# A logarithm in SBUF, its add on GpSimd, and the front's steps placed anew in a selective-scan loop

## The chip, the cores and the metric

The kernel runs on one core of a Trainium2 chip. A core has a matrix engine (TensorE, PE in the profile; PEld are its weight loads), VectorE (DVE), ScalarE (ACT), GpSimd (POOL) and SyncE (SP), which here issues most of the DMAs. Each engine works through its own queue in order; engines wait for each other through semaphores. The metric is the device time of one execution in microseconds.

## The reference

The whole program is a two-layer model; the part that the change touches is the Mamba block of the first layer. For each of four groups of 64 channels (`nb`) and each of four images (`b`) it computes, over 1024 positions:

```
xz = xs @ inw.T
u, z = jnp.split(xz, 2, axis=-1)
u = silu(causal depthwise conv of u, 4 taps)
xdbc = u @ xpw.T
dt = softplus(xdbc[..., :4] @ dtw.T + dtb)
Bm, Cm = xdbc[..., 4:20], xdbc[..., 20:36]
dA  = exp(dt[..., None] * A)
dBu = (dt * u)[..., None] * Bm[:, :, None, :]
h_t = dA_t * h_(t-1) + dBu_t ;  y_t = sum over 16 states of h_t * C_t ;  y = y + u * D
out = y * silu(z) @ outw.T
```

There are 128 inner channels with 16 states each. Everything behind it (gates, depthwise convolutions, attention, a second attention layer, a mixture of experts) is the same in both kernels.

## The kernel before, in words

The work is cut into 16 blocks, one for each pair of group and image, in the order of `order` (all groups of image 0, then image 1, and so on). A block has 128 channels x 16 states = 2048 recurrences, and a tile has 128 partitions, so a block is 16 steps; in one step eight channels with their 16 states fill the partitions and the 1024 positions lie along the free axis. The loop runs over `t` from 0 to 259; `n = t // 16` is the block and `j = t % 16` the step.

One step does this:

- SP loads `dA` (`fetch`, L905): eight rows of dt from DRAM, each spread over 16 partitions. There are five buffers; the load for step t+4 is issued in step t.
- ScalarE takes its exponential in place (`decay`, L910), three steps ahead.
- TensorE writes dt*u, spread in the same way, into one of two PSUM buffers `dBu` (`select`, L917), two steps ahead. dt*u is held as three bf16 parts in `U`.
- VectorE multiplies it by B (L975) and runs the recurrence with `tensor_tensor_scan` (L978) into `hs`, which has six buffers.
- GpSimd multiplies `hs` by C (L979).
- TensorE sums over the states into `pY` (`add_up`, L928 for steps 0, 1, 14 and 15 of a block, L935 for pairs of the others, L941 for u*D), three steps behind. `pY` is a PSUM tile of 4 KB per partition, and its pool has one buffer: the first sum of a block (step 0's, issued in step 3 of the block) is the first write to the tile in which the block before collected its result.

Around these steps the loop places the work of other blocks. `front(n)` returns the steps that prepare block n, each with a number: a step with number i >= 0 is issued in step i of block n-1, one with i < 0 in step 16+i of block n-2. They are: the projection and convolution as matmuls (`project`, four parts, L484), `silu` (L488), the matmul for dt (`project_dt`, L495), softplus in pieces that avoid a large exponential (`exps`: Abs, Relu, Exp, and 1+e into the PSUM tile, L500 to L503; `rest`: VectorE's correction, L506, and GpSimd's subtraction, L507; `log`, L510; `dt_out`: the last add, L513, the store of dt to DRAM, L515, and e = dt*u, L516), the three bf16 parts of dt*u (`part1`, `part2`, L520 to L526), B and C spread over the partitions by matmul and copied by ScalarE (`spread`, L542 and L544), the store of the parts (`parts_out`, L530) and their load in another layout (`turn`, L537).

The loop itself also places the work on block n-1's result: `gated` (ScalarE copies `pY` into `u`, L566), `times_gate` (GpSimd multiplies by silu(z), L569), `project_out` (L579, L580), `store` (L585), and for block n `gate` (silu(z), L557 and L559). `module_gate` and `module` (L598 to L614) apply a gate to finished images.

PSUM is full during the loop: two `dBu` buffers, one `pY` and one buffer called `mm`, which all the other matmuls share in turn, of two banks each. The order of the instructions on every engine is the order in which the loop issues them (`tc.manual_schedule`); semaphores come from the tiles' reads and writes, and a tile's buffer passes on to the next tile of its name when all who read or write the old one are done. Ahead of the loop a planner (`Plan`) interleaves the normalisation and block 0's own front; it also issues the first five steps of front 1. Its list of engines, costs and keys decides the order there.

Of the kernel before, what the change touches and what calls it, by code (L numbers as in the profile page):

```python
# [10 lines left out]
F32 = mybir.dt.float32  # L11
BF16 = mybir.dt.bfloat16
AF = mybir.ActivationFunctionType
ALU = mybir.AluOpType
# [4 lines left out]
N = HH * WW  # L19
NP = N + 2  # L20
P = 128
CT = C // P
NT = N // P
NB, DM, DIN, DS, DTR, K = 4, 64, 128, 16, 4, 4
# [371 lines left out]
def body(tc, g, out):  # L396
    nc = tc.nc
    act, mm = nc.scalar.activation, nc.tensor.matmul
    ts, tt, stt = nc.vector.tensor_scalar, nc.vector.tensor_tensor, nc.vector.scalar_tensor_tensor
# [6 lines left out]
    with pool("const", 1) as cp, pool("dram", 1, space=bass.MemoryType.DRAM) as drp, contextlib.ExitStack() as late:  # L406
# [16 lines left out]
        def V(name, j=0, n=1):  # L423
            return vec[:, VOFF[name] + j : VOFF[name] + j + n]
# [26 lines left out]
        order = [(nb, b) for b in range(B) for nb in range(NB)]  # L451
        NBLK = NJ * len(order)
        with pool("mconst", 1) as mc, pool("front", 1) as fp, pool("dts", 2, space=bass.MemoryType.DRAM) as dsp, pool(
            "mps", 1, space=PSUM
        ) as mps:
            m_cu = mc.tile([P, CT, K, DIN], F32, tag="m_cu", name="m_cu")
# [8 lines left out]
            def block(nb, b):  # L465
                q0 = (nb % 2) * DM
                return slice(q0, q0 + DM), XM[b][q0 : q0 + DM, nb // 2]

            def big():
                return mps.tile([P, N], F32, tag="mm", name="mm")  # L470

            def front(n):


                nb, b = order[n]
                rows_in, xb = block(nb, b)
                r = state[n] = {}

                def project(part):
                    if part == 0:  # L480
                        r["pu"] = big()
                    h = HALVES[part // 2]
                    for k in range(part % 2 * 2, part % 2 * 2 + 2):
                        mm(r["pu"][:, h], m_cu[rows_in, nb // 2, k], xb[:, k + h.start : k + h.stop], start=k == 0, stop=k == K - 1)  # L484

                def silu():
                    r["u"] = fp.tile([P, N], F32, tag="u", name="u", bufs=3)
                    act(r["u"], r["pu"], AF.Silu, bias=V("convb", nb), scale=1.0)  # L488

                def project_dt():
                    r["pdt"] = big()
                    for h in HALVES:
                        mm(r["pdt"][:, h], m_wdt[:, nb, :], r["u"][:, h], start=True, stop=True)  # L495

                def exps():
                    e = r["e"] = fp.tile([P, N], F32, tag="e", name="e")
                    dt = r["dt"] = fp.tile([P, N], F32, tag="dt", name="dt")
                    act(e, r["pdt"], AF.Abs, bias=V("dtb", nb), scale=1.0)  # L500
                    act(dt, r["pdt"], AF.Relu, bias=V("dtb", nb), scale=1.0)
                    act(e, e, AF.Exp, scale=-1.0)
                    act(r["pdt"], e, AF.Identity, bias=one, scale=1.0)  # L503

                def rest():
                    stt(r["e"], r["pdt"], -1.0, r["e"], ALU.add, ALU.subtract)  # L506
                    nc.gpsimd.tensor_tensor(r["dt"], r["dt"], r["e"], ALU.subtract)  # L507

                def log():
                    act(r["pdt"], r["pdt"], AF.Ln)  # L510

                def dt_out():
                    tt(r["dt"], r["dt"], r["pdt"], ALU.add)  # L513
                    r["ds"] = dsp.tile([NJ, DB, N], F32, tag="ds", name="ds")
                    nc.sync.dma_start(out=r["ds"].rearrange("j d n -> (j d) n"), in_=r["dt"])  # L515
                    nc.gpsimd.tensor_tensor(r["e"], r["dt"], r["u"], ALU.mult)  # L516

                def part1():
                    p = r["parts"] = fp.tile([P, 3, N], BF16, tag="parts", name="parts")
                    nc.scalar.copy(p[:, 0], r["e"])  # L520
                    nc.gpsimd.tensor_tensor(r["e"], r["e"], p[:, 0], ALU.subtract)

                def part2():
                    p = r["parts"]
                    nc.scalar.copy(p[:, 1], r["e"])
                    nc.gpsimd.tensor_tensor(p[:, 2], r["e"], p[:, 1], ALU.subtract)  # L526

                def parts_out():
                    dq = r["dq"] = dsp.tile([P, 3, N], BF16, tag="dq", name="dq")
                    nc.sync.dma_start(out=dq, in_=r["parts"])  # L530

                def turn():

                    dq = r["dq"]
                    U = r["U"] = fp.tile([96, 4, N], BF16, tag="U", name="U", bufs=2)
                    for q in range(3):
                        nc.sync.dma_start(out=U[32 * q : 32 * q + 32], in_=dq.rearrange("(t c) q n -> q c t n", c=32)[q])  # L537

                def spread(c):
                    p = big()  # L540
                    for h in HALVES:
                        mm(p[:, h], m_bc[:, nb, c * P : (c + 1) * P], r["u"][:, h], start=True, stop=True)  # L542
                    t = r["BC"[c]] = fp.tile([P, N], F32, tag=f"bc{c}", name=f"bc{c}", bufs=2)
                    nc.scalar.copy(t, p)  # L544

                return [(i - 5, lambda i=i: project(i)) for i in range(4)] + [
                    (-1, silu), (0, project_dt), (1, exps), (3, rest), (4, log), (5, dt_out), (6, part1),
                    (6, lambda: spread(0)), (7, part2), (7, lambda: spread(1)), (10, parts_out), (12, turn),
                ]

            def gate(n):
# [66 lines left out]
            with pool("scan", 6) as sp, pool("yps", 1, space=PSUM) as yps, pool("dps", 2, space=PSUM) as dps, pool("lnA", 1) as wp:  # L618
# [50 lines left out]
                def XN(b, ks=range(CT), hs=range(2)):  # L669
                    return [("xn", b, k, h) for k in ks for h in hs]  # L670
# [272 lines left out]
                fronts = [front(n) for n in range(1, len(order))]  # L943
                fronts = [None] + fronts
# [15 lines left out]
                with pre.beside(-1, -1, -1, low=True):  # L960
                    for b in range(1, B):
                        normalise(b)
                    for i, step in fronts[1]:
                        if i < 0:
                            add("PE" if i < -1 else "ACT", 1720 if i < -1 else 1150, step, XN(0, [0]) + ["m_cu"], ["mm"])

                with tc.manual_schedule():
                    pre.run()
                with tc.manual_schedule():
                    for t in range(NBLK + 4):  # L970
                        n, j = t // NJ, t % NJ
                        if t < NBLK:
                            r = state[n]
                            dBu = dBus.pop(t)
                            tt(dBu, dBu, r["B"], ALU.mult)  # L975

                            hs = hss[t] = sp.tile([P, N], F32, tag="hs", name="hs")
                            nc.vector.tensor_tensor_scan(hs, dAs.pop(t), dBu, 0.0, ALU.mult, ALU.add)  # L978
                            nc.gpsimd.tensor_tensor(hs, hs, r["C"], ALU.mult)  # L979
                        if j == 3 and n > 0:  # L980
                            gated(n - 1)
                        select(t + 2)
                        add_up(t - 3)
                        fetch(t + 4)
                        decay(t + 3)
                        for ahead in (1, 2):
                            if n + ahead < len(order):
                                for i, step in fronts[n + ahead]:
                                    if i == j - (ahead - 1) * NJ:
                                        step()  # L990
                        for i, step in behind:
                            if i == t:
                                step()
                        if 0 < n < len(order) and j == 4:
                            times_gate(n - 1)
                        last = n == len(order)
                        for i in range(2):
                            if n > 0 and j == (3 if last else 8 + i):
                                project_out(n - 1, i)
                        if n > 0 and j == (3 if last else 9):  # L1000
                            store(n - 1)
                        if not last and j == 10:
                            gate(n)
                        if n > NB and j == 5 and n % NB > 0:
                            module_gate(n // NB - 1, n % NB - 1)
                        if n > NB and j == 8 and n % NB > 1:
                            module(n // NB - 1, n % NB - 2)


# [12 lines left out]
        with pool("sets", 1) as wp, pool("work", 1) as kp, pool("ps2", 1, space=PSUM) as ps:  # L1022
# [45 lines left out]
            add = plan.add  # L1068
# [1044 lines left out]
```

## Time and profile before

| what | value |
|---|---|
| median of the runs | 2809.41 us (2807.25 to 2810.01, 3 runs) |
| profiled execution | 2797.35 us, span of its instructions 2795.4 us |
| mean granted TensorE clock | 0.966 |
| busy over the span | PE 2525.0, DVE 2018.1, ACT 1540.3, POOL 1285.7 us |
| first scan of block 0, 1, 15 | 89.42, 157.75, 994.14 us |
| blocks 1 to 14, first scan to first scan | 836.39 us, mean 59.74, shortest 58.69 |
| L513 (the add that is moved) | 15 times, 1.19 us each |
| landing of a DMA, median | dA 4.7, ds 3.0, parts 5.8, U 5.9 us |

A line of a group is: source line, engine, operation, what it writes and reads, how often, then busy time and mean duration in ns, then the idle time of the engine just before and who ended it. A line of the order in time is: start and length in us, engine, source line, operation, and in square brackets the idle time before it with its releaser. A line of waits is: who waited for whom, us in total, times, longest. A line of stretches is: start and end, length, then busy time and number of instructions of PE, PEld, DVE, ACT and POOL, then granted clock, share of DMA time and GB/s.

### The profile page before, as it was taken

What the parts mean: (1) busy time and instruction counts of PE and PEld (TensorE: products, weight loads), DVE (VectorE), ACT (ScalarE), POOL (GpSimd) and SP (SyncE); (2) the same over time, 40 slices, a digit from 0 to 9 for tenths busy, and PEclk for the clock granted to TensorE, in tenths of its full rate; (3) what the DMA queues carried; (4) which work ended last, traced back from release to release, by engine and by line L of the source; (5) the groups of instructions that cost most, each with busy time, mean ns of one, the idle gap of its engine ahead of it and who ended that gap; (6) DMA issues with size and microseconds to landing.
All of it is one profiled execution on the core that took longest, in us unless ns stands there. A gap on an engine that the chain in (4) does not pass through costs nothing. (4 is left out here: it accounts for less than half of the span.)

```text
span 2795.4 us, 38909 instructions
## 1 busy us (share of the span) xinstructions
PE 2525.0 (90%) x15320; PEld 1490.3 (53%) x15320; DVE 2018.1 (72%) x2276; ACT 1540.3 (55%) x2082; POOL 1285.7 (46%) x807
## 2 busy tenths in 40 slices
PE   7788888888888878999899999998999997999996
PEld 5322222222222223676655656664666676899996
DVE  6899999999999996877995997777594566111112
ACT  4766666766676743776875975775443433111110
POOL 1688788887887870000010020012343436666652
PEclk9989999999999989999999999999999999999998
DMA  4667766776666653000001000000000013555546
GB/s 147 158 164 183 174 168 179 185 184 168 173 173 173 183 133 106 5 9 22 22 1 39 8 3 9 9 17 16 1 16 8 8 32 116 181 140 140 127 98 181
DMA packets 95433, 269.58 MB, mean 96 GB/s; under 512 B 18694, under 2 KB 36726, under 8 KB 91920
## 3 DMA queue, kind: packets, MB, share of 16 engines
q1 hardware_dynamic: 66560, 202.52, 27.3%
q0 software_dynamic: 26512, 60.35, 8.4%
q10 hardware_dynamic: 2176, 4.19, 0.4%
q8 instruction: 122, 2.00, 0.3%
q14 instruction: 63, 0.52, 0.1%
HBM read 291.57 MB, written 42.80 MB: 120 GB/s over the span
## 5 line engine op out<-in xcount | busy, mean ns | idle before, releaser
L979 POOL TENSOR_TENSOR hs<-hs,bc 128x1024 f32<-128x1024 f32 x256 | 600.8, 2354 | 157.7 <-DVE hs L978 154.1
L978 DVE TENSOR_TENSOR_SCAN hs<-dA,dBu 128x1024 f32<-128x1024 f32 x256 | 585.4, 2287 | 37.1 <-PE pY L935 6.8
L1321 DVE TENSOR_REDUCE nm<-s 128x1 f32<-128x1024 f32 x256 | 301.5, 1218 | 93.0 <-PE s L1312 91.5
L910 ACT ACTIVATE dA<-dA,aneg 128x1024 f32<-128x1024 f32 x256 | 286.6, 1144 | 96.5 <-DMA dA<-ds 81.6
L1326 ACT ACTIVATE pr<-s,nm 128x1024 f32<-128x1024 f32 x256 | 285.4, 1121 | 96.0 <-DVE nm L1321 71.2
L975 DVE TENSOR_TENSOR dBu<-dBu,bc 128x1024 f32<-128x1024 f32 x256 | 309.8, 1210 | 10.3 <-PE dBu L917 10.3
L1390 POOL TENSOR_TENSOR b<-b 128x1024 f32<-128x1024 f32 (+1 forms) x15 | 29.6, 1971 | 591.1 <-ACT b L1386 591.1
L1340 PE MATMUL k<-const,pr 128*128 128x128 f32 x2048 | 270.3, 279 | 21.5 <-ACT pr L1326 6.2
L1340 PEld LDWEIGHTS k<-const,pr 128*128 128x128 f32 x2048 | 226.4, 142 | 110.8 <-issue 49.4
L917 PE MATMUL dBu<-U,pick 96*128 96x512 bf16 x512 | 160.5, 397 | 113.9 <-DVE hs L978 113.7
L1988 PE MATMUL s<-pT,b 128*128 128x128 f32 x1920 | 231.2, 277 | 6.3 <-DMA b<-we,intse 5.8
L1988 PEld LDWEIGHTS s<-pT,b 128*128 128x128 f32 x1920 | 227.0, 193 | 11.5 <-issue 6.0
L935 PE MATMUL pY<-hs,const 128*32 128x512 f32 x768 | 215.0, 687 | 0.0
L1992 DVE TENSOR_TENSOR pT<-pT,s 128x512 f32<-128x512 f32 x72 | 49.3, 685 | 229.3 <-ACT pT L1991 229.1
L917 PEld LDWEIGHTS <-pick 96*128 96x128 bf16 x512 | 40.3, 98 | 290.2 <-issue 170.7
L1344 ACT COPY pT<-k 128x512 f32<-128x512 f32 x288 | 156.5, 597 | 51.4 <-PE k L1340 51.1
L1344 DVE COPY pT<-k 128x512 f32<-128x512 f32 x224 | 144.9, 682 | 34.0 <-PE k L1340 31.8
L1312 PE MATMUL s<-b,b 32*128 32x512 f32 x512 | 166.6, 644 | 0.7 <-ACT pr L1326 0.6
L1312 PE MATMUL s<-b,qs 32*128 32x512 f32 x512 | 166.6, 644 | 0.0
L1360 PEld LDWEIGHTS k<-pT,b 128*32 128x32 f32 x4096 | 108.0, 111 | 58.2 <-issue 26.8
L928 PE MATMUL pY<-hs,const 128*128 128x512 f32 x256 | 122.3, 600 | 12.2 <-ACT u L566 9.0
L1360 PE MATMUL k<-pT,b 128*32 128x128 f32 x4096 | 130.2, 276 | 3.0 <-DVE pT L1344 3.0
(485 smaller groups left out, 4636.3 us busy)
## 6 DMA issues: line engine op xcount, KB each, us to landing
dA<-ds SPq DMA_DIRECT2D x256, 512.0 KB, 4.7
dq<-parts SPq DMA_DIRECT2D x15, 768.0 KB, 5.8
U<-dq SPq DMA_DIRECT2D x45, 256.0 KB, 5.9
ds<-dt SPq DMA_DIRECT2D x16, 512.0 KB, 3.0
b<-x SPq DMA_DIRECT2D x4, 1024.0 KB, 6.6
acc<-pr SPq DMA_DIRECT2D x8, 512.0 KB, 8.6
qs<-b SPq DMA_DIRECT2D x32, 128.0 KB, 2.2
xm<-x SPq DMA_DIRECT2D x4, 1024.0 KB, 5.2
```

The source lines that it names most:

```text
L910: act(dAs[t], dAs[t], AF.Exp, scale=aneg[:, c : c + 1])
L935: mm(r["pY"][32 * q : 32 * q + 32, h], strip[:, P - DB - i * DB : P - i * DB + 32 - DB], hs[:, h], start=False, stop=False,)
L975: tt(dBu, dBu, r["B"], ALU.mult)
L978: nc.vector.tensor_tensor_scan(hs, dAs.pop(t), dBu, 0.0, ALU.mult, ALU.add)
L979: nc.gpsimd.tensor_tensor(hs, hs, r["C"], ALU.mult)
L1312: mm(S[i][:, HALVES[h]], q, kT[rr, HALVES[h]], start=True, stop=True)
L1321: "DVE", 1130, lambda i=i, u=u: nc.vector.tensor_reduce(nms[u], S[i], AX.X, ALU.max, negate=True),
L1326: "ACT", 1100, lambda i=i, u=u, hd=hd: act(prs[u % 4], S[i], AF.Exp, bias=nms[u], scale=1.0, accum_out=rss[b % 2][:, k, qt, hd : hd + 1]), ...
L1340: nc.tensor.transpose(bank.t[:, j * P : (j + 1) * P], prs[u][:, c0 : c0 + P], ident)
L1344: 470, 598, lambda dst=dst, bank=bank: nc.scalar.copy(dst, bank.t), lambda dst=dst, bank=bank: nc.vector.tensor_copy(dst, bank.t),
L1360: mm(bank.t[i * HD : (i + 1) * HD, 0:P], v[:, 4 * jh + j, hd * HD : (hd + 1) * HD], pTs[m][jh][:, i, j * P : (j + 1) * P], start=(jh, j) = ...
L1988: mm(p12[:, a, c], wbufs[w][:, o : o + P], xT[:, k], start=k == 0, stop=k == CT - 1)
```

## The change

The logarithm no longer overwrites its PSUM tile. It writes into SBUF, into the memory of the `parts` tile of the same front, read as float32; that tile is now created in `log` and not in `part1`. The add of the logarithm to dt goes from VectorE to GpSimd, which can read it there. And the steps are placed anew:

| step | before | after |
|---|---|---|
| project, four parts | -5, -4, -3, -2 | -3, -3, -2, -1 |
| project_dt | 0 | 1 |
| rest | 3 | 4 |
| spread(0), spread(1) | 6, 7 | 7, 10 |
| turn | 12 | 11 |
| gated (not in the tail of the loop) | 3 | 5 |
| times_gate | 4 | 5 |
| project_out, two halves | 8, 9 | 9, 9 |
| gate | 10 | 11 |
| module | 8 | 13 |

`silu` (-1), `exps` (1), `log` (4), `dt_out` (5), `part1` (6), `part2` (7), `parts_out` (10), `store` (9) and `module_gate` (5) keep their steps. The planner is given the first five steps of front 1 by their place in the list instead of by their negative numbers, with the same engines and costs.

```diff
 def log():
-    act(r["pdt"], r["pdt"], AF.Ln)
+    r["parts"] = fp.tile([P, 3, N], BF16, tag="parts", name="parts")
+    r["ln"] = r["parts"].rearrange("p q n -> p (q n)").bitcast(F32)[:, :N]
+    act(r["ln"], r["pdt"], AF.Ln)

 def dt_out():
-    tt(r["dt"], r["dt"], r["pdt"], ALU.add)
+    nc.gpsimd.tensor_tensor(r["dt"], r["dt"], r["ln"], ALU.add)
     r["ds"] = dsp.tile([NJ, DB, N], F32, tag="ds", name="ds")
...
 def part1():
-    p = r["parts"] = fp.tile([P, 3, N], BF16, tag="parts", name="parts")
+    p = r["parts"]
...
-return [(i - 5, lambda i=i: project(i)) for i in range(4)] + [
-    (-1, silu), (0, project_dt), (1, exps), (3, rest), (4, log), (5, dt_out), (6, part1),
-    (6, lambda: spread(0)), (7, part2), (7, lambda: spread(1)), (10, parts_out), (12, turn),
+return [((-3, -3, -2, -1)[i], lambda i=i: project(i)) for i in range(4)] + [
+    (-1, silu), (1, project_dt), (1, exps), (4, rest), (4, log), (5, dt_out), (6, part1),
+    (7, lambda: spread(0)), (7, part2), (10, lambda: spread(1)), (10, parts_out), (11, turn),
 ]
...
-for i, step in fronts[1]:
-    if i < 0:
-        add("PE" if i < -1 else "ACT", 1720 if i < -1 else 1150, step, XN(0, [0]) + ["m_cu"], ["mm"])
+for i, (_, step) in enumerate(fronts[1][:5]):
+    add("PE" if i < 4 else "ACT", 1720 if i < 4 else 1150, step, XN(0, [0]) + ["m_cu"], ["mm"])
...
-if j == 3 and n > 0:
+last = n == len(order)
+if n > 0 and j == (3 if last else 5):
     gated(n - 1)
 select(t + 2)
 add_up(t - 3)
...
-if 0 < n < len(order) and j == 4:
+if 0 < n < len(order) and j == 5:
     times_gate(n - 1)
-last = n == len(order)
 for i in range(2):
-    if n > 0 and j == (3 if last else 8 + i):
+    if n > 0 and j == (3 if last else 9):
         project_out(n - 1, i)
 if n > 0 and j == (3 if last else 9):
     store(n - 1)
-if not last and j == 10:
+if not last and j == 11:
     gate(n)
 if n > NB and j == 5 and n % NB > 0:
     module_gate(n // NB - 1, n % NB - 1)
-if n > NB and j == 8 and n % NB > 1:
+if n > NB and j == 13 and n % NB > 1:
     module(n // NB - 1, n % NB - 2)
```

## The prediction

> **What bounds the kernel now.** I read the costliest groups of the page first, then the busy time by stretches over the scan loop, then the waits inside it, then three engines' instructions in order of time through one block. A block is one (module, image) pair of sixteen steps; I number blocks 0 to 15 and steps 0 to 15. Scans of step 0 start blocks 1 and 15 at 157.75 and 994.14 us.
>
> ```profile
> L979 POOL TENSOR_TENSOR hs<-hs,bc 128x1024 f32<-128x1024 f32 x256 | 600.8, 2354 | 157.7 <-DVE hs L978 154.1
> L978 DVE TENSOR_TENSOR_SCAN hs<-dA,dBu 128x1024 f32<-128x1024 f32 x256 | 585.4, 2287 | 37.1 <-PE pY L935 6.8
> ```
> ```profile
> 278.60:337.29 58.69, 48.81 (x141) 15.54 (x140) 56.83 (x35) 38.20 (x36) 48.51 (x22) 0.97 0.72 179
> 157.75:994.14 836.39, 713.34 (x1997) 224.83 (x1996) 796.86 (x477) 566.49 (x516) 695.22 (x304) 0.95 0.69 176
> ```
>
> The second fence is busy time of PE, PEld, DVE, ACT, POOL, then granted clock. VectorE is busy 56.83 us of the 58.69 us of block 3, and 797 of 836 us in blocks 1 to 14: it sets the pace. GpSimd waits for its scans, not the other way round. Now block 9, VectorE:
>
> ```profile
> 639.87 2.29 DVE L978 TENSOR_TENSOR_SCAN hs<-dA,dBu 128x1024 f32<-128x1024 f32 x1
> ...
> 655.14 2.29 DVE L978 TENSOR_TENSOR_SCAN hs<-dA,dBu 128x1024 f32<-128x1024 f32 x1
> 657.35 1.20 DVE L513 TENSOR_TENSOR dt<-dt,mm 128x1024 f32<-128x1024 f32 x1
> 658.46 1.23 DVE L975 TENSOR_TENSOR dBu<-dBu,bc 128x1024 f32<-128x1024 f32 x1
> 659.72 2.29 DVE L978 TENSOR_TENSOR_SCAN hs<-dA,dBu 128x1024 f32<-128x1024 f32 x1
> ```
>
> The first scan is step 1's and ends at 642.16. Undisturbed scans start 3.54 us apart (639.87, 643.41). Sixteen steps are 56.64; block 3 has 2.05 more, for L506 (+1.10) and L513, the add that the change removes: 655.14 to 659.72 is 4.58, 1.04 over a plain step, and the step behind it takes 3.44, so the add costs 0.94.
>
> ScalarE and TensorE in the same block:
>
> ```profile
> 643.11 1.11 ACT L500 ACTIVATE e<-mm,vec 128x1024 f32<-128x1024 f32 x1 [0.88 <-PE mm L495]
> ...
> 646.21 1.12 ACT L503 ACTIVATE mm<-e,one 128x1024 f32<-128x1024 f32 x1
> ...
> 648.30 0.99 ACT L566 COPY u<-pY 128x1024 f32<-128x1024 f32 x1
> 649.19 2.43 ACT L910 ACTIVATE dA<-dA,aneg 128x1024 f32<-128x1024 f32 x2
> 651.64 1.28 ACT L510 ACT_TABLE_LOAD   x1
> 652.94 1.01 ACT L510 ACTIVATE mm<-mm 128x1024 f32<-128x1024 f32 x1
> ```
> ```profile
> 639.19 1.91 PE L935 MATMUL pY<-hs,const 128*32 128x512 f32 x8
> 641.03 1.98 PE L495 MATMUL mm<-u,m_wdt 128*128 128x512 f32 x4
> ...
> 649.30 0.61 PE L917 MATMUL dBu<-U,pick 96*128 96x512 bf16 x2 [1.24 <-DVE hs L978]
> 649.74 1.88 PE L928 MATMUL pY<-hs,const 128*128 128x512 f32 x4
> 651.46 1.02 PE L941 MATMUL pY<-u,ddiag 128*128 128x512 f32 x2
> 653.94 0.59 PE L917 MATMUL dBu<-U,pick 96*128 96x512 bf16 x2 [1.46 <-DVE hs L978]
> ```
>
> The L928 at 649.74 is step 0's sum, issued in step 3. It is the first write to the new block's pY, and pY has one buffer: it may only start once the copy L566 has read the old block's pY. That the wait is real is in the waits of blocks 1 to 14:
>
> ```profile
> PE pY L928 <- ACT u L566: 9.0, 7, 1.6
> ```
>
> Last, what a pause does to TensorE (block 8), with the clock of that stretch as the last column but two:
>
> ```profile
> 600.51 0.61 PE L917 MATMUL dBu<-U,pick 96*128 96x512 bf16 x2 [3.97 <-DVE hs L978]
> 601.04 3.58 PE L935 MATMUL pY<-hs,const 128*32 128x512 f32 x8
> ```
> ```profile
> 601.00:604.40 3.40, 3.40 (x9) 0.56 (x8) 3.37 (x3) 1.04 (x1) 3.40 (x3) 0.51 0.64 170
> ```
>
> After a pause of 3.97 us the eight matmuls that take 1.91 us at 639.19 take 3.58, at clock 0.51. The clock records show a slow stretch of 3.4 or 6.8 us behind every one of the six such pauses (blocks 1 to 4, 8, 12).
>
> **The change, part by part.**
>
> *The add leaves VectorE.* 0.94 us in each of blocks 0 to 14. The floor of a block falls from 58.69 to 57.75.
>
> *The add on GpSimd.* One more operation of the form of L507 (2.35) per block. GpSimd then has 48.5 + 2.35 = 51 us in 57.75. In steps 4 to 7 it has four products (9.4) and six others (four at 2.35, two at 2.14: 13.7), 23.1 against 15.3 of VectorE, so it falls up to 8 us behind; a product is wanted three steps after its scan (10.6 less its own 2.35). Nothing on the path as long as that 8.3 us lead lasts. The dt store on SP waits for this add. VectorE's add ends 1.1 us after step 5's scan (658.55); on GpSimd it comes behind that step's product, 2 x 2.35 = 4.8 after it: 3.7 us later, and so do the dA loads queued behind the store. Step 10's exponential was done 4.3 us ahead of its scan (mean of blocks 1 to 14), so 0.6 us remains, more if VectorE is held up earlier. [...]
>
> *The logarithm into SBUF.* Nearest rows: 1.01 (L510, PSUM to PSUM) and 1.11 (L500, PSUM to SBUF): 0 to 0.1 us on ScalarE; I take 0. It no longer waits for L506. Table loads stay the same in number.
>
> *Moves that stay hidden.* The first projection is packed into steps 13 to 15: TensorE has 3.9 to 4.0 us of work in steps 13 and 14, 2.2 in 15 and 0, against 3.54, so it is at most 1 us late and the selections are two steps ahead; at half clock that cover is gone and step 14 can lose 2.7 us, as blocks 8 and 12 did. `spread`, `project_out`, `gate`, `module` move by one to five steps; their readers sit at least three steps later, and B and C are first read in the next block. `turn` waits on SP for the parts' store (5.8 us to landing) one step sooner, and the next dA load wants SP two steps after that store, 7.1 us: nothing. `times_gate` at step 5 is read at step 9. The five early steps of front 1 keep order and prices. All 0; the bound is the 14.7 us of stalls that blocks 1 to 14 have now (836.4 less 14 x 58.69), lost or kept: I take them as gone, because the next item gives every queue time.
>
> *The copy of pY moves from step 3 to step 5, and its wait stays in step 3.* The new pY's first matmul still stands in TensorE's queue at step 3. ScalarE's queue now reads: step 1 the four operations of `exps`, decays of steps 5, 6, 7, table load, logarithm, copy. And `project_dt`, which `exps` needs, moves from step 0 to 1. From the end of step 1's scan (642.16 in block 9) as zero:
> - TensorE: selection at 0.06, first sum at 0.49, its four passes 1.72 (649.74 to 651.46), `project_dt` 1.98: ends 4.19. ScalarE starts 0.10 later, 4.29.
> - `exps` 4.22 (643.11 to 647.33): 8.5. Three decays 3.3 (2.43 is two with a gap): 11.8. Load 1.28, logarithm 1.01: 14.1. Copy 0.99: 15.1. The dA load for step 7 lands at 3.54 + 4.7 = 8.2, so it isn't last.
> - TensorE resumes at 15.2; step 0's sum and its ddiag 2.6; selection of step 6 0.6, behind them in the queue: 18.4.
> - VectorE wants that selection at 16.30 (658.46) less 1.10 for the removed add: 15.2.
>
> So VectorE stands 3.2 us before step 6 of every block with a front (1 to 14). TensorE has done its selection at 7.8 and pauses until 15.2: 7.4 us. That is nearly twice 3.97, and each 3.97 brought half clock. A slow stretch lasts 3.4 to 6.8 us, so the 2.6 us of sums take 1.7 to 2.6 longer, and the selection up to 0.4. I take +2.4, stall 5.6; ends 3.2 (no slow stretch) and 6.2.
>
> Block 15 has no `exps` and no logarithm: from step 2's end the load lands at 4.7, decay 1.15, copy 1.0, sums and selection 3.3: 10.2, wanted at 10.5. Nothing, or some 3 us at half clock.
>
> **Sum.** Blocks 1 to 14: 14 x (57.75 + 5.6) = 886.9 against 836.4: +50.5. Block 0: -0.9. About +49.6. The rest of the span starts from the end of the loop and moves with it. The profiled execution is 2797.35 us (span 2795.4, 2 around it), 12 below the median of the runs, so the sum gives 2847 there and 2859 on the median.
>
> **Rivals.**
> *The hold is covered: faster.* If the copy ended by 11.9 instead of 15.1, step 6's selection would be there in time and only the removed add would count: 15 x 0.94 = -14 us, up to -28 if all present stalls go too; 2790. For it: VectorE is the bound and the matmuls now wait only 9 us for that copy. Against it: the logarithm alone ended 11.8 us after step 1's scan in block 9 with `project_dt` a step earlier.
> *Held, but at full clock.* Stall 3.2: 14 x 60.95 = 853.3, +17, less 0.9: 2825. For it: many blocks run whole at clock 1.00. Against: the pause is 7.4.
> *GpSimd becomes the bound.* If waits for ScalarE's casts (20 us over 14 blocks) push its lag from 8 to 12 us, TensorE's sums come some 2 us late a block: +28 - 14: 2823. VectorE's stall speaks against it.
> *The two cancel.* The forecast crosses zero at a stall of 2.1 us; 1.7 to 2.5 stays within 0.2%. It needs the chain 1.1 us shorter and no slow clock.
>
> **How the numbers follow.** Within 0.2% (5.6 us) I call the time unchanged: the three runs lie 0.1% apart. Chances: held with slow clock 0.74, with its own range 2840 to 2885 (stall 4.3, to 6.2 with the 14.7 us of other stalls kept and block 15's 3); full clock 0.09; GpSimd 0.04; cancel 0.05; covered 0.08. The first three are slower. The range goes from the full-clock case to 2880.
>
> **What would show it.** L566's copy starting about 14 us behind step 1's scan; TensorE idle over 7 us before L928, named by ACT u; VectorE idle some 5.6 us before step 6's L975, named by PE; clock 0.5 there in each block; blocks 63 us apart; block 15's first scan at 1044 us where it was at 994. Wrong if the first L928 does not wait (then about 2790), or if the pause leaves the clock at 1.0.

## The result and the profile after

The changed kernel takes 2856.56 us (median of 6 runs, 2850.11 to 2858.56). The kernel before, run beside it, takes 2809.71 us (6 runs, 2802.65 to 2815.42). The ratio is 1.0163, 95% interval 1.0146 to 1.0181: 47 us slower. The forecast was 2859, so the size came out within 3 us. The profiled execution is 2858.56 us with a span of 2856.6 us, at a mean clock of 0.954 (before: 0.966).

Line numbers are 1 or 2 higher than before: the scan is now L979, the multiplication by B L976, the product by C L980, the selection L919, the decay L912, the sums L930 and L937, u*D L943, the logarithm L512, the moved add L515, the copy of `pY` L568.

The costliest groups of the page, for the lines that say most:

```profile
L980 POOL TENSOR_TENSOR hs<-hs,bc 128x1024 f32<-128x1024 f32 x256 | 600.6, 2355 | 157.0 <-DVE hs L979 156.1
L979 DVE TENSOR_TENSOR_SCAN hs<-dA,dBu 128x1024 f32<-128x1024 f32 x256 | 585.2, 2286 | 36.9 <-PE pY L937 3.0
...
L976 DVE TENSOR_TENSOR dBu<-dBu,bc 128x1024 f32<-128x1024 f32 x256 | 309.4, 1208 | 74.5 <-PE dBu L919 74.5
```

The durations per instruction are what they were. What has grown is the idle time of VectorE ahead of L976: 74.5 us, all of it put down to the selection on TensorE (10.3 us on the page of before). GpSimd still waits 156 us for scans, so it isn't the bound, with the moved add on it.

Stretches of block 9 (the first line) and of blocks 1 to 14 (the second): busy time of PE, PEld, DVE, ACT and POOL, then clock, DMA share and GB/s.

```profile
662.65:725.64 62.99, 51.66 (x149) 17.35 (x148) 55.80 (x34) 40.55 (x38) 50.85 (x23) 0.95 0.65 167
157.36:1041.75 884.39, 700.70 (x2002) 233.77 (x2001) 781.17 (x462) 567.26 (x517) 728.61 (x318) 0.93 0.65 166
```

VectorE has less to do than before (781 us against 797 in blocks 1 to 14), and takes longer over it: 884.39 us against 836.39. A block is 63.17 us on average where it was 59.74. VectorE is busy 55.80 of 62.99 us in block 9: seven idle us in a block of the engine that sets the pace.

The waits in the same stretch, in us, times and longest, name the chain of two links:

```profile
POOL hs L980 <- DVE hs L979: 120.6, 109, 1.3
PE pY L930 <- ACT u L568: 101.1, 14, 7.6
DVE dBu L976 <- PE dBu L919: 71.6, 14, 5.7
```

Each of the last two stands there 14 times, once a block. Before, TensorE waited 9.0 us in all for that copy. Block 9 in order of time, VectorE first:

```profile
666.20 2.29 DVE L979 TENSOR_TENSOR_SCAN hs<-dA,dBu 128x1024 f32<-128x1024 f32 x1
...
681.50 2.29 DVE L979 TENSOR_TENSOR_SCAN hs<-dA,dBu 128x1024 f32<-128x1024 f32 x1
688.42 1.23 DVE L976 TENSOR_TENSOR dBu<-dBu,bc 128x1024 f32<-128x1024 f32 x1 [4.64 <-PE dBu L919]
```

ScalarE:

```profile
672.68 1.11 ACT L500 ACTIVATE e<-mm,vec 128x1024 f32<-128x1024 f32 x1 [2.68 <-PE mm L495]
...
675.77 1.12 ACT L503 ACTIVATE mm<-e,one 128x1024 f32<-128x1024 f32 x1
676.83 3.21 ACT L912 ACTIVATE dA<-dA,aneg 128x1024 f32<-128x1024 f32 x3
680.06 1.28 ACT L512 ACT_TABLE_LOAD   x1
681.35 1.02 ACT L512 ACTIVATE parts<-mm 128x1024 f32<-128x1024 f32 x1
682.27 1.01 ACT L568 COPY u<-pY 128x1024 f32<-128x1024 f32 x1
```

TensorE:

```profile
675.62 0.60 PE L919 MATMUL dBu<-U,pick 96*128 96x512 bf16 x2 [0.89 <-DVE hs L979]
683.42 3.67 PE L930 MATMUL pY<-hs,const 128*128 128x512 f32 x4 [7.19 <-ACT u L568]
686.93 1.02 PE L943 MATMUL pY<-u,ddiag 128*128 128x512 f32 x2
687.79 0.60 PE L919 MATMUL dBu<-U,pick 96*128 96x512 bf16 x2
```

Step 1's scan ends at 668.49. ScalarE works without a gap from 672.68 to 683.28, and the copy, last of these in its queue, starts 13.79 us behind that scan. TensorE ends the selection of 675.62 and from then on stands at step 0's sum, with the next selections queued behind it: 7.19 us. Then the four passes of that sum take 3.67 us where they took 1.88 (the first L928 row that the forecast shows), since the clock is at 0.50. This is the stretch of the passes (PE, PEld, DVE, ACT, POOL, clock, DMA share, GB/s):

```profile
683.40:686.90 3.50, 3.48 (x4) 1.50 (x5) 0.38 (x1) 2.33 (x2) 3.48 (x3) 0.50 0.00 0
```

VectorE finished step 5's scan at 683.79 and gets step 6's selection at 688.39.

The loop gives the whole difference. The first scan of block 0 starts at 89.67 us (before 89.42), that of block 15 at 1041.75 (before 994.14), and the last scan ends at 1098.45 (before 1050.48): 48.0 us later. The two medians are 47 us apart. The two profiled executions are 61 us apart; the other 13 us lie behind the loop, where no edit was made (1758.1 us from the last scan to the end, 1745.0 before). Before's profiled execution was 12 us below its own median. The kernels of the next section show how far this part varies without an edit: 1754 to 1759 us in four profiles on one chip, 1740 to 1748 us in six on two others. On which chip the two profiled executions above were made is not on record, and what varies there was not pursued.

### The profile page after: what moved, and what is told of

Same layout as the page of the kernel before. It is cut to its first block, busy times and chain, and to the rows that moved or that the text cites. A ratio compares the mean times of both kernels' runs of the same rounds, so it can differ in the third digit from the quotient of the medians.

```text
span 2856.6 us, 38954 instructions
## 1 busy us (share of the span) xinstructions
PE 2522.4 (88%) x15320; PEld 1504.0 (53%) x15320; DVE 2002.8 (70%) x2261; ACT 1540.1 (54%) x2082; POOL 1321.2 (46%) x822
## 3 DMA queue, kind: packets, MB, share of 16 engines
q0 software_dynamic: 26512, 60.35, 8.3%
## 5 line engine op out<-in xcount | busy, mean ns | idle before, releaser
L980 POOL TENSOR_TENSOR hs<-hs,bc 128x1024 f32<-128x1024 f32 x256 | 600.6, 2355 | 157.0 <-DVE hs L979 156.1
L979 DVE TENSOR_TENSOR_SCAN hs<-dA,dBu 128x1024 f32<-128x1024 f32 x256 | 585.2, 2286 | 36.9 <-PE pY L937 3.0
L976 DVE TENSOR_TENSOR dBu<-dBu,bc 128x1024 f32<-128x1024 f32 x256 | 309.4, 1208 | 74.5 <-PE dBu L919 74.5
L912 ACT ACTIVATE dA<-dA,aneg 128x1024 f32<-128x1024 f32 x256 | 285.5, 1143 | 62.5 <-DMA dA<-ds 57.8
L919 PE MATMUL dBu<-U,pick 96*128 96x512 bf16 x512 | 158.9, 393 | 97.9 <-DVE hs L979 97.9
L930 PE MATMUL pY<-hs,const 128*128 128x512 f32 x256 | 148.1, 708 | 106.8 <-ACT u L568 103.6
L1989 PEld LDWEIGHTS s<-pT,b 128*128 128x128 f32 x1920 | 227.8, 193 | 12.6 <-issue 7.0
L919 PEld LDWEIGHTS <-pick 96*128 96x128 bf16 x512 | 39.0, 99 | 290.7 <-DVE hs L979 144.0
L937 PE MATMUL pY<-hs,const 128*32 128x512 f32 x768 | 191.2, 620 | 0.0
L930 PEld LDWEIGHTS pY<-hs,const 128*128 128x128 f32 x256 | 54.3, 220 | 162.0 <-issue 147.4
```

The source lines that it names most:

```text
L912: act(dAs[t], dAs[t], AF.Exp, scale=aneg[:, c : c + 1])
L919: mm(dBus[t][:, h], pick[:, j % 4], state[t // NJ]["U"][:, j // 4, h], start=True, stop=True)
L930: mm(r["pY"][:, h], strip[:, P - DB - j * DB : 2 * P - DB - j * DB], hs[:, h], start=p == 0, stop=p == NJ - 1)
L1989: mm(p12[:, a, c], wbufs[w][:, o : o + P], xT[:, k], start=k == 0, stop=k == CT - 1)
```

## The experiments

The theory is the forecast's: the copy's place in ScalarE's queue holds TensorE at the first write to the single `pY`, and the pause halves the clock. The rivals: something else among the moves or GpSimd does it; the hold does it alone, without the clock. The runs were made on three chips, each beside the kernel before on the same chip (2808.52, 2798.15 and 2796.56 us), so they are compared by ratios and by the loop's blocks.

### The copy back at step 3 (a_copy3)

```diff
-if n > 0 and j == (3 if last else 5):
+if n > 0 and j == 3:
     gated(n - 1)
```

> The changed kernel with the copy of pY back at step 3; everything else of the change stays. Theory (TensorE's first sum of a block is held by the late copy, then runs at half clock): the copy then stands behind the decay of step 5 alone, ends 10.4 us after step 1's scan, TensorE resumes at 10.6, the selection of step 6 is there between 13.9 (full clock) and 16.5 (half clock) where 15.2 is wanted: VectorE stands 0 to 1.3 us instead of 5.2, blocks 57.8 to 59.1 us, time 2780 to 2798 us, faster than both. Rival (the other moves or GpSimd's extra add starve VectorE, the copy is innocent): still 2840 or more.

2794.21 us against 2808.52 (ratio 0.9950, 0.9934 to 0.9967). A block takes 58.86 us on average. The place of one copy in ScalarE's queue turns the change from 47 us slower to 14 faster. All other moves and GpSimd's add are still in this kernel, and 14 is what the removed add is worth (b_ln below), so the other moves cost nothing that shows in the sum. The theory holds. The waits over the same 14 blocks (156.39 to 980.46 us), and the first sum of the block that answers to block 9 above:

```profile
PE pY L930 <- ACT u L568: 38.8, 14, 2.8
DVE dBu L976 <- PE dBu L919: 7.3, 13, 1.6
```
```profile
645.76 3.01 PE L930 MATMUL pY<-hs,const 128*128 128x512 f32 x4 [2.77 <-ACT u L568]
```

TensorE still waits up to 2.8 us a block, and the passes still take 3.01 us instead of 1.88. But the copy ends 10.4 us behind step 1's scan where it was 14.8, and VectorE's wait for selections is down to 7.3 us in all.

### The copy alone moved in the old kernel (b_copy5)

```diff
-if j == 3 and n > 0:
+if n > 0 and j == (3 if n == len(order) else 5):
     gated(n - 1)
...
-if 0 < n < len(order) and j == 4:
+if 0 < n < len(order) and j == 5:
     times_gate(n - 1)
```

> The kernel before with only the copy of pY at step 5 (and the multiplication by silu(z) behind it, at step 5 too). The logarithm ends 11.8 us after step 1's scan, the copy 12.8, TensorE resumes at 12.9; at full clock the selection of step 6 is there at 16.1 where 16.3 is wanted. Theory with slow clock: the pause of TensorE is over 5 us, so the sums behind it run at half clock, 1.7 to 3.0 us later: VectorE stands 1.5 to 2.8 us in blocks 1 to 14, time 2830 to 2849 us. Theory of the hold at full clock: no stall, 2810 us within 6.

2836.86 us against 2808.52 (ratio 1.0102, 1.0084 to 1.0120): 28 us slower by this edit alone. In the old kernel `project_dt` is at step 0, so the copy ends 12.3 to 13.2 us behind step 1's scan. That is 28 us in a kernel whose chain, at full clock, should have cost next to nothing (the next run has one block that shows it at full clock, with a stall of 0.26 us). TensorE pauses 4.7 to 5.6 us, the clock is 0.5 behind each of the fourteen pauses, and VectorE waits 0.9 to 2.7 us before step 6. The block takes 61.73 us. Its row in block 9:

```profile
671.90 3.75 PE L928 MATMUL pY<-hs,const 128*128 128x512 f32 x4 [5.04 <-ACT u L566]
675.45 1.91 PE L941 MATMUL pY<-u,ddiag 128*128 128x512 f32 x2
677.15 0.99 PE L917 MATMUL dBu<-U,pick 96*128 96x512 bf16 x2
```

### The same hold, with TensorE kept busy (b_copy5_warm)

As b_copy5, and step 5's selection is issued nine times, each writing the same values over the last, so that TensorE works while it would stand.

```diff
-mm(dBus[t][:, h], pick[:, j % 4], state[t // NJ]["U"][:, j // 4, h], start=True, stop=True)
+for again in range(9 if t >= NJ and t % NJ == 5 else 1):
+    mm(dBus[t][:, h], pick[:, j % 4], state[t // NJ]["U"][:, j // 4, h], start=True, stop=True)
```

> The kernel b_copy5 with the selection of step 5 issued nine times over in step 3 of each block from block 1 on (the same values written again, before VectorE reads them): 3.4 us of matmuls that fill the pause of TensorE down to under 2 us. Theory with slow clock: the clock stays at 1.0, step 6's selection is there in time, 2810 us within 6. If the later copy itself costs the time and not the clock, it stays where b_copy5 is.

2816.75 us (ratio 1.0029, 1.0018 to 1.0039), 20 us below b_copy5, with more work on TensorE and the copy just as late. It ends 8.2 us above the kernel before, 2 above what was expected. Ten blocks have a pause of 1.2 to 2.2 us, clock 1.0 behind it and no stall, or 0.26 us in block 9. Blocks 3, 7, 11 and 13 have a pause of about 2.16 us, half clock behind it, and VectorE waits some 2 us. Block 10, one of the ten:

```profile
712.33 4.06 PE L918 MATMUL dBu<-U,pick 96*128 96x512 bf16 x18 [1.24 <-DVE hs L979]
718.06 1.96 PE L929 MATMUL pY<-hs,const 128*128 128x512 f32 x4 [1.67 <-ACT u L566]
```

The passes take 1.96 us with the sum issued as late as in b_copy5. Blocks 9 and 11 are alike up to there but for the clock: in both TensorE pauses 2.16 us, and the copy ends 13.22 us behind step 1's scan. The first sum and the multiplication of step 6, block 9 and then block 11:

```profile
657.19 1.95 PE L929 MATMUL pY<-hs,const 128*128 128x512 f32 x4 [2.16 <-ACT u L566]
660.48 1.23 DVE L976 TENSOR_TENSOR dBu<-dBu,bc 128x1024 f32<-128x1024 f32 x1 [0.26 <-PE dBu L918]
...
777.25 2.77 PE L929 MATMUL pY<-hs,const 128*128 128x512 f32 x4 [2.16 <-ACT u L566]
782.23 1.23 DVE L976 TENSOR_TENSOR dBu<-dBu,bc 128x1024 f32<-128x1024 f32 x1 [1.96 <-PE dBu L918]
```

The clock is 1.0 behind the pause of block 9 and 0.5 from 778.26 on in block 11. So the half clock behind the pause is what decides in that kernel, and the rival without it falls.

### The logarithm and GpSimd's add alone, old steps (b_ln)

```diff
-act(r["pdt"], r["pdt"], AF.Ln)
+r["parts"] = fp.tile([P, 3, N], BF16, tag="parts", name="parts")
+r["ln"] = r["parts"].rearrange("p q n -> p (q n)").bitcast(F32)[:, :N]
+act(r["ln"], r["pdt"], AF.Ln)
...
-tt(r["dt"], r["dt"], r["pdt"], ALU.add)
+nc.gpsimd.tensor_tensor(r["dt"], r["dt"], r["ln"], ALU.add)
...
-p = r["parts"] = fp.tile([P, 3, N], BF16, tag="parts", name="parts")
+p = r["parts"]
```

> The kernel before with the logarithm into SBUF and its add on GpSimd alone; all steps as before. Theory: 15 x 0.94 = 14 us faster than before, 2795 us within 6, if the small stalls of before stay as they are.

2785.73 us against 2798.15 (ratio 0.9951, 0.9933 to 0.9969; 0.0049 of 2809 is 13.8 us). The undisturbed block takes 57.77 us; the forecast's floor was 57.75. So the first half of the change is worth what its 0.94 us a block said, where VectorE doesn't stand waiting anyway.

GpSimd's products start at most 6.4 to 7.4 us behind the end of their scans in twelve of blocks 1 to 14, inside the 8.3 us lead. In blocks 1 and 5 they are 10.3 and 10.5 us late, beyond it. Block 1 was like that before (9.8). In block 5 GpSimd also clears a tile for the gate of finished images, once in the program, and that now stands behind the moved add. ScalarE waits for it, TensorE waits for ScalarE, and VectorE stands 5.69 us where it stood 0.92:

```profile
425.43 1.01 ACT L603 ACTIVATE xs<-mm 4x1024 f32<-4x1024 f32 x1 [8.87 <-POOL xs L596]
428.65 3.41 PE L544 MATMUL mm<-u,m_bc 128*128 128x512 f32 x4 [6.07 <-ACT xs L603]
432.52 1.23 DVE L977 TENSOR_TENSOR dBu<-dBu,bc 128x1024 f32<-128x1024 f32 x1 [5.69 <-PE dBu L919]
```

The forecast put the add on GpSimd at nothing. That holds where the lead does; block 5 takes 63.77 us here (60.35 before) and 63.51 in a_copy3.

### The changed kernel with the add back on VectorE

From SBUF (a_add_dve):

```diff
-nc.gpsimd.tensor_tensor(r["dt"], r["dt"], r["ln"], ALU.add)
+tt(r["dt"], r["dt"], r["ln"], ALU.add)
```

> The changed kernel with the add of the logarithm on VectorE again (reading it from SBUF); all steps as in the change. Theory: VectorE does that add in step 5 and then waits for step 6's selection anyway, so the add is hidden in the stall: 2857 us within 6, VectorE's idle time before step 6's multiplication 1.1 us shorter. Rival (the moved add gains 0.94 us a block whatever else happens, as in a sum of parts): 14 us slower than the change, 2870.

From PSUM, as the kernel before has it (a_add_psum); the three edits of b_ln are undone in the changed kernel, and the steps stay new:

```diff
-nc.gpsimd.tensor_tensor(r["dt"], r["dt"], r["ln"], ALU.add)
+tt(r["dt"], r["dt"], r["pdt"], ALU.add)
```

> The changed kernel with the logarithm and its add as they were before (in PSUM, on VectorE); all steps as in the change. Theory: VectorE's add of 1.2 us falls into the wait for step 6's selection and costs nothing: the same time as the change (2856.6 beside 2809.7, ratio 1.016) within 6 us, VectorE's idle time before step 6's multiplication about 1.1 us shorter than the 4.5 to 5.7 of the change. Rival: 14 us slower than the change, ratio 1.021.

a_add_dve: 2859.16 us (ratio 1.0183, 1.0165 to 1.0201), blocks of 63.11 us. a_add_psum: 2848.48 us against 2796.56 (ratio 1.0191, 1.0174 to 1.0208), blocks of 63.18 us. The changed kernel has 63.17. The ratio of a_add_psum lies midway between what theory and rival expected; its loop, where the edit is, is as long as that of the changed kernel (941.0 against 941.1 us from block 1's first scan to the last scan's end), and the rest was not pursued. In block 9 of a_add_psum, on VectorE, the add stands in the time in which VectorE would wait:

```profile
684.60 1.22 DVE L513 TENSOR_TENSOR dt<-dt,mm 128x1024 f32<-128x1024 f32 x1 [0.16 <-POOL dt L507]
689.20 1.23 DVE L974 TENSOR_TENSOR dBu<-dBu,bc 128x1024 f32<-128x1024 f32 x1 [3.38 <-PE dBu L917]
```

The idle time ahead of step 6 is 3.1 to 4.6 us there, 4.5 to 5.7 in the changed kernel. What the change takes off VectorE comes back as idle time of the same step: in this kernel the removal is worth nothing.

One thing was missed. In a_add_dve the idle time fell by 3.3 us on average and not by 1.2: the add reads both inputs from SBUF and takes 3.41 us.

### `project_dt` back at step 0

With the copy at step 5 (a_dt0):

```diff
-(-1, silu), (1, project_dt), (1, exps), (4, rest), (4, log), (5, dt_out), (6, part1),
+(-1, silu), (0, project_dt), (1, exps), (4, rest), (4, log), (5, dt_out), (6, part1),
```

> The changed kernel with project_dt at step 0; the copy stays at step 5. Theory: exps end 3.3 us sooner, but the decay of step 7 then waits for its load (8.3), so the logarithm ends at 11.7 and the copy at 12.6 instead of 14.8; TensorE resumes at 12.8 after a pause of 5 us, still at half clock: step 6's selection at 17.7 to 18.6 where 15.2 is wanted, VectorE stands 2.5 to 3.4 us, blocks 60.3 to 61.2, 2815 to 2832 us. At full clock the stall would be 0.7 us and the time 2790 us.

2820.35 us against 2798.15 (ratio 1.0078, 1.0061 to 1.0096), blocks of 61.46 us, stalls of 3.2 to 3.5 us: `project_dt`'s step accounts for about 1.7 of the 5.1 us in a block. The block lies 0.3 us above what was expected, as the copy ended 13.7 us behind step 1's scan, not 12.6. ScalarE shows why:

```profile
666.11 1.02 ACT L512 ACTIVATE parts<-mm 128x1024 f32<-128x1024 f32 x1 [1.40 <-DVE e L506]
```

The logarithm waits 1.40 us for VectorE's L506, which the forecast had said it no longer does.

With the copy at step 3 too (a_dt0_copy3, both edits in the changed kernel):

> The changed kernel with the copy of pY at step 3 and project_dt at step 0, as they were before; all else of the change stays. Theory: exps end 5.2 us after step 1's scan, the copy 7.1, before TensorE has done step 5's selection (7.7): no pause, no slow clock, VectorE's floor of 57.75 us a block with only the small stalls at other steps: blocks 57.8 to 58.4, 2778 to 2790 us, some 8 us faster than the change with the copy alone moved back. If the slow clock has no part in that kernel's remaining stalls, no faster than it (2794).

2776.97 us against 2798.15 (ratio 0.9918, 0.9899 to 0.9937): faster than both kernels, and 21 us below the kernel before on the same chip. Most blocks take 57.80 us. Block 9 in the view of stretches, and the waits:

```profile
628.30:686.11 57.81, 50.39 (x149) 16.69 (x148) 55.69 (x33) 41.47 (x39) 50.81 (x23) 1.00 0.73 182
```
```profile
PE pY L930 <- ACT u L568: 3.5, 4, 1.3
DVE dBu L976 <- PE dBu L919: 2.1, 3, 1.2
```

VectorE is busy 55.69 of 57.81 us, and the clock is 1.00. The mean block is 58.51: single stalls remain (3.1 us in block 5, step 9; 2.5 in step 10; 2.0 in block 3, step 0). GpSimd's products come up to 7.9 us late there, at the edge of their lead, but 9.6 in block 1 and 11.7 in block 5, where ScalarE and TensorE wait for the same clearing as in b_ln.

In that kernel no stall covers the add, so its price can be read. With the add on VectorE from PSUM (a_dt0_copy3_psum, edits as in a_add_psum) and from SBUF (a_dt0_copy3_dve, edit as in a_add_dve):

> The changed kernel with project_dt at step 0, the copy at step 3, and the logarithm and its add as before (in PSUM, on VectorE). It tells apart why the same add on VectorE, read from SBUF, took 3.4 us instead of 1.2. If it is the second SBUF operand beside GpSimd's work, the add takes 1.2 us here and the kernel is 14 us slower than the one with the add on GpSimd (ratio to before 0.997, blocks 58.7 to 59.4). If it is the later subtraction on GpSimd that VectorE waits for, the loss stays near 46 us (ratio 1.008).

> The same with the add of the logarithm on VectorE. Theory: with no hold in step 6 the add costs VectorE its 0.94 us in each of 15 blocks: 14 us slower than with the add on GpSimd, 2792 to 2804 us. Rival (GpSimd's extra operation costs as much as it saves): the same time as with the add on GpSimd.

From PSUM: 2790.73 us against 2796.56 (ratio 0.9981, 0.9971 to 0.9992), as expected; the usual block is 59.03 us, 1.23 above 57.80, and the add takes 1.22. That is 0.3 us above the price of 0.94 that the kernel before showed; why was not pursued. From SBUF: 2822.73 us against 2798.15 (ratio 1.0087, 1.0069 to 1.0105), 46 us above a_dt0_copy3 where 14 were expected; the block is 61.24. VectorE and GpSimd of the latter:

```profile
671.52 3.41 DVE L515 TENSOR_TENSOR dt<-dt,parts 128x1024 f32<-128x1024 f32 x1 [0.17 <-POOL dt L507]
```
```profile
669.13 2.35 POOL L507 TENSOR_TENSOR dt<-dt,e 128x1024 f32<-128x1024 f32 x1
671.49 2.35 POOL L980 TENSOR_TENSOR hs<-hs,bc 128x1024 f32<-128x1024 f32 x1
```

Both adds wait for GpSimd's subtraction by some 0.17 us, so that isn't the difference; the second input in SBUF is. The add ends 1.1 us after GpSimd's product (674.93 against 673.84), one undisturbed add later: it looks as if it stood still while GpSimd ran. Block 8 of the same run has the other order. There GpSimd starts its product 0.27 us behind the add, not just ahead of it:

```profile
612.51 1.23 DVE L515 TENSOR_TENSOR dt<-dt,parts 128x1024 f32<-128x1024 f32 x1 [0.17 <-POOL dt L507]
612.78 3.16 POOL L980 TENSOR_TENSOR hs<-hs,bc 128x1024 f32<-128x1024 f32 x1 [0.30 <-issue]
```

The same add takes 1.23 us, and it is the product that takes 0.8 us longer. a_add_dve has the same exception in block 8 (1.22 and 3.17 us). So two inputs in SBUF are not slow in themselves: in these blocks the add and GpSimd's product overlap, and the one that started second took longer, the add 3.41 us instead of 1.23, or the product 3.16 instead of 2.35.

## Why the prediction was right

*The mechanism.* Each link was found where the forecast put it: the copy starts 13.79 us behind step 1's scan (said: about 14), TensorE pauses 7.19 us (7.4), the clock is 0.5 behind the pause in all 14 blocks, VectorE idles 5.12 us on average before step 6 (5.6), blocks are 63.17 us apart (63.35), and block 15's first scan starts at 1041.75 (1044). a_copy3 shows that the loss goes with the copy's place, b_copy5 that this place alone makes one.

*The chain to the copy.* Predicted end 15.1, measured 14.80. `exps` started at 4.20 (4.29 said) and the logarithm ended at 13.89 (14.1 said): no term is off by more than 0.2 us.

*The slow clock.* From the first sum to the end of u*D: 2.74 us at full clock by the rows (the forecast added up 2.6), 4.35 to 5.46 in the changed kernel, 4.95 on average: 2.2 us more, where 2.4 was taken from bounds of 1.7 to 2.6. The stalls alternate between some 4.5 and 5.6 us. In the trace the changes of the granted clock lie whole multiples of 3.413 us apart, and 63.17 is 18.5 times that, so every second block meets the pause half a multiple further on: this fits, and was not tested.

*The add's 0.94.* Right as a price, as b_ln shows; and added up rightly, as the stall was worked out from the time at which VectorE, now without the add, wants the selection. a_add_psum shows that this gain was lost inside the stall.

*The small stalls.* They were taken as gone. Of 14.7 us in blocks 1 to 14, 2.7 were left. With 71.6 before step 6 and 14 undisturbed blocks of 57.80 (809.2) this makes 883.5 of the 884.39 measured. The forecast had 886.9, and part of that agreement is luck: the stall was 0.48 us a block shorter than said, 6.7 us in all, and the small stalls and a floor 0.05 us higher gave most of it back.

*The ends of the loop.* Block 0 took 67.7 us (68.3 before; -0.9 was said, -0.6 measured). Block 15 took 56.7 (56.3 before): it waited 1.1 us before step 6, between the two values named.

*GpSimd.* In the changed kernel the latest product of a block starts 5.1 us behind its scan in the median block, and 7.3 at most; up to 8 were named. Without VectorE's stall it is later (a_copy3: 7.4 us, and 11.0 in block 5): the stall lets it catch up, as the rival's own sentence said. The add takes 2.35 us on GpSimd (b_ln) where it took 1.19 on VectorE, and that difference was rightly given no price: in b_ln the same move is a gain, as the 2.35 us lie beside VectorE's work.

*What was wrong.* "It no longer waits for L506." The logarithm reads the PSUM tile that L506 reads, and a_dt0 shows it waiting 1.40 us for L506. In the changed kernel L506 ended at 680.22 and the table was loaded at 681.34, so the sentence changed no number.

## What to carry to other kernels

A read that frees a single buffer has to be placed by the first write of the next user in the writer's queue: everything queued behind that write waits with it, whatever it has to do with the buffer. Work taken off the engine that sets the pace is worth nothing in a step where that engine already waits for something else; undo the wait first (a_copy3: 62 us from the place of one copy), then the removal pays (b_ln and a_dt0_copy3). A pause of the matrix engine can cost twice, once as time and once as clock (block 9 of the changed kernel: 7.19 us, then 3.67 us at clock 0.50 for four passes that took 1.88 at full clock). Work moved to an engine with time to spare on average can still arrive late in the one block where that engine has more to do (block 5 of b_ln).

## What the hardware did that was not expected

*Half clock behind a pause of 2.16 us.* The forecast for b_copy5_warm had the clock at 1.0 behind pauses of under 2 us. In the trace of before, the changes of the granted clock lie whole multiples of 3.413 us apart; call the stretches of that length windows. Between 140 and 1060 us TensorE was busy 0.39 or less in 16 windows, and the clock was 0.5 in the window behind each of them. There are 20 stretches of half clock: 15 came behind such windows, and five behind windows busy 0.76 to 0.83, though 33 windows as busy as that had full clock behind them. Where full clock returned, the window before was busy 0.93 or more. The trace of the changed kernel has 31 windows busy 0.35 or less in the same stretch, each with half clock behind it. Pauses before the first sum were followed by half clock in 14 of 14 blocks of the changed kernel (7.1 to 7.6 us) and of b_copy5 (4.7 to 5.6 us); pauses of 2.16 us were in four blocks of b_copy5_warm and were not in a fifth, block 9. What differs there is where the pause lies among the windows: it left one busy 0.37 in each of the four, and one busy 0.47 in block 9.

*An add with two SBUF inputs beside GpSimd.* With both inputs in SBUF (a_dt0_copy3_dve) the add took 3.41 us on VectorE in block 9, where GpSimd's product started just ahead of it, and 1.23 us in block 8, where it started ahead of the product. With one input in PSUM (a_dt0_copy3_psum) it took 1.22 us all 15 times. So the logarithm's new place and the add's new engine belong together in this kernel: with the logarithm in SBUF, leaving the add on VectorE (a_dt0_copy3_dve) is 30 us slower than leaving both in PSUM (a_dt0_copy3_psum): 24.6 above its kernel before against 5.8 below.
